# The last tile of a routed expert kernel: its sum and store in three parts instead of two, and two early stores joined

## The chip, the cores and the metric

The kernel runs on one core of a Trainium2 chip. The metric is the device time of one execution in microseconds (us); the profile's own times are given in us from the start of its span, single instructions also in nanoseconds (ns). Engines are called as in the profile: PE (TensorE, matmuls), PEld (its weight loads), DVE (VectorE), ACT (ScalarE), POOL (GpSimd) and SP (SyncE, which only issues transfers here). SPq and ACTq are the queues on which SP and ACT issue transfers (DMAs).

## The reference

`x` is 128 batches of 32 tokens with 128 features, float32. First each batch gets a linear layer of its own, a mix of 8 masked matrices; then 2 of 8 experts are chosen per batch, and one shared expert is applied to every token. Both layers are added to their input.

```python
w_bot = einsum('bg,got->bot', cond, weight * mask)
x = x + einsum('bnt,bot->bno', x, w_bot) + bias
# per batch: softmax over cond, the best 2 of 8 experts, weights normalised
out = sum over experts e of we[:, e] * mlp(x, gate[e], up[e], down[e])
out = out + mlp(x, shared_gate, shared_up, shared_down)
x = x + out
# mlp(x, g, u, d) = (gelu(x @ g) * (x @ u)) @ d, hidden width 512
```

## The kernel before

All arrays lie with the features on the 128 partitions and the 4096 tokens along the free axis, as 8 tiles of 512 columns (`TB`); `P` is 128. `x1` holds the output of the first layer, `acc` the running sum of the second one, both with all 4096 columns. The order of work is written out by hand (`manual_schedule`), so that each engine executes its instructions in the order of the code; buffers come from pools that hand them out in turn, and an instruction that takes a buffer again waits until the earlier user of it is done.

The kernel first builds the 128 matrices of the batches and applies them, with the routing computed on DVE beside it. Then it runs MLP tiles: two shared tiles, 27 expert tiles whose tokens are gathered by POOL and whose sums are scattered into `acc` by DVE (L716), and at the end the remaining shared tiles 2 to 7. More expert tiles than 27 are in a branch of `tc.If` (L822); the profiled execution loads 27 sets of expert weights, so it took the `Else` branch, in which `late_tiles` (L807) follows at once. Both branches hold a copy of `late_tiles`.

A shared tile has 4 groups of 128 hidden units. For each, `hidden` (L574) issues the gate and the up matmul (L580, 512 columns each), a GELU on ACT (L585) and a product on DVE (L587) that gives `h`; `down` (L590) multiplies `h` by the down weights into a PSUM bank `ps_out` (L598), accumulating over the 4 groups. `Pipeline.run` (L649) keeps `down` one group behind `hidden`, so that PE has the next group's matmuls while ACT and DVE make `h`; for the last tile the lag is set to 2 (L815). With a lag of 2, the groups 2 and 3 of the last tile are still pending when `run` returns, and the loop behind it issues their `down` matmuls, part by part.

A tile may be given `widths`: then its output columns are cut into parts with a PSUM bank each. The pool `ps_o` (L84) has three banks. When a part's last group is done, `finish` (L659) is called. For shared tiles above number 2 it takes a buffer `o` from a pool of two, adds the bank and `acc` into it on DVE (L668), and stores it (L670):

```python
o_pool = ctx.enter_context(tc.tile_pool(name="o", bufs=2))      # L79
...
o = o_pool.tile([P, w], F32, name="o", tag="o")                 # L667
nc.vector.tensor_tensor(o, ps[:, 0:w], acc[:, cols], ALU.add)
queue = nc.scalar if part.start else nc.sync
queue.dma_start(out=outT[:, cols], in_=o)
```

So tiles 3 to 6 take one `o` buffer each, and the last tile, number 7, takes one for each part: 384 columns, stored on SP's queue, and 128 columns, stored on ACT's. The finished tiles 0 to 2 lie in `acc` itself and are stored from there at the top of `late_tiles`, by two transfers on SP's queue (L810): 1024 columns, and the 512 of tile 2, whose last addition (L665) comes some microseconds later. After that, SP's queue has only the stores of `o`.

At the very end each engine runs through its branch (L822), and SP waits for the last stores (L885).

Of the kernel before, what the change touches and what calls it, by code (L numbers as in the profile page):

```python
# [25 lines left out]
EARLY = 2  # L26
# [4 lines left out]
def kernel(  # L31
# [16 lines left out]
    nc = tc.nc  # L48
    P = 128
# [5 lines left out]
    TB = 512  # L55
    BT = TB // N
    NTILE = NT // TB
# [47 lines left out]
    def warm_up(n):  # L105
# [10 lines left out]
        out=before,  # L116
        in_=ones,
# [38 lines left out]
    acc = const.tile([P, NT], F32, name="acc")  # L156
# [499 lines left out]
    pipe = Pipeline(h_pool)  # L656

    def shared_tile(t, widths=None):
        def finish(ps, part):  # L659
            w = part.stop - part.start  # L660
            cols = slice(t * TB + part.start, t * TB + part.stop)
            if t < EARLY:
                nc.vector.tensor_tensor(acc[:, cols], ps[:, 0:w], x1[:, cols], ALU.add)
            elif t == EARLY:
                nc.vector.tensor_tensor(acc[:, cols], ps[:, 0:w], acc[:, cols], ALU.add)  # L665
            else:
                o = o_pool.tile([P, w], F32, name="o", tag="o")  # L667
                nc.vector.tensor_tensor(o, ps[:, 0:w], acc[:, cols], ALU.add)  # L668
                queue = nc.scalar if part.start else nc.sync
                queue.dma_start(out=outT[:, cols], in_=o)  # L670

        return Mlp(TB, x1[:, ts(t, TB)], shared, finish, widths)
# [133 lines left out]

    def late_tiles(pipe):  # L807
        late.ps = None
        for early in (slice(0, EARLY * TB), ts(EARLY, TB)):
            nc.sync.dma_start(out=outT[:, early], in_=acc[:, early])  # L810
        pipe.run(late, slice(1, None))
        for t in range(EARLY + 2, NTILE - 1):
            pipe.run(shared_tile(t))

        pipe.lag = 2  # L815
        pipe.run(shared_tile(NTILE - 1, (TB - P, P)))
        for part in range(2):
            for mlp, group, h in pipe.pending:
                mlp.down(group, h, slice(part, part + 1))


    with tc.If(n_used > SURE[0], preferred_fallthrough_block=False) as more_tiles:  # L822
        more = Pipeline(h_more_pool)
        for kind in range(3):
            for i in range(SURE[kind], CAPS[kind]):
                more.run(expert_tile(more, kind, i))
        more.drain()
        more.flush()
        late_tiles(pipe.copy())
    with more_tiles.Else():  # L830
        late_tiles(pipe)
# [57 lines left out]
```

## Time and profile before

| what | value |
|---|---|
| median of 3 runs | 285.92 us (285.91 to 286.01) |
| the profiled execution's own time | 285.23 us |
| its span, first to last instruction | 283.3 us |
| mean granted TensorE clock | 0.998 of full |
| PE busy, share of the span | 278.0 us, 98% |
| DVE, ACT, POOL busy | 167.0, 78.9 and 48.1 us |
| transfers | 27.21 MB, of them 2.10 MB written |

The profiled execution took 1.93 us more than its span, which lies ahead of the first and behind the last instruction, and was 0.69 us shorter than the median of the timed runs. In the profile, a matmul in float32 appears as two instructions of PE (and two weight loads), so "x2" of a form is one matmul of the code. "To landing" is the time from the issue of a transfer until its completion is signalled.

### The profile page before, as it was taken

To read this page: it belongs to the slowest core of one execution; us is meant where nothing else is said; L and a number is where in the kernel's file an instruction comes from. 1 tells how busy PE (TensorE), PEld (TensorE's weight loads), DVE (VectorE), ACT (ScalarE), POOL (GpSimd) and SP (SyncE) were. 2 spreads that over 40 slices of the span, in tenths; PEclk is the share of its full clock that TensorE was granted. 3 is DMA by queue.
4 is the path that set the end of the run, shared out by engine and by line. 5 is a ranking of instruction groups with operands and counts; after the bars stand their busy time and mean duration, and the time that the engine had idled before them with its cause. 6 is when DMAs were issued, how large, how long until landed. Compare 5 with 4: busy or idle time off the path is not lost. (4 is left out here: it accounts for less than half of the span.)

```text
span 283.3 us, 5170 instructions
## 1 busy us (share of the span) xinstructions
PE 278.0 (98%) x1424; PEld 172.1 (61%) x1424; DVE 167.0 (59%) x489; ACT 78.9 (28%) x149; POOL 48.1 (17%) x285
## 2 busy tenths in 40 slices
PE   8999999999999999999999999999999999999994
PEld 7987545657657567576675665765557444444442
DVE  4897794546666666666566676666666833233232
ACT  5665123222222222222222222222222222222220
POOL 3001213423024220241222212421000000000000
PEclk9999999999999999999999999999999999999999
DMA  4381068434335335325353343432000020100001
GB/s 121 116 207 58 2 167 278 115 111 118 113 106 170 127 111 150 113 93 167 82 186 106 112 150 111 126 118 94 3 0 1 25 86 0 39 37 11 26 37 46
DMA packets 25763, 27.21 MB, mean 96 GB/s; under 512 B 1920, under 2 KB 16768, under 8 KB 25728
## 3 DMA queue, kind: packets, MB, share of 16 engines
q1 hardware_dynamic: 25440, 26.42, 30.5%
q10 hardware_dynamic: 288, 0.39, 0.5%
q8 instruction: 13, 0.21, 0.3%
q14 instruction: 22, 0.18, 0.2%
HBM read 24.71 MB, written 2.10 MB: 95 GB/s over the span
## 5 line engine op out<-in xcount | busy, mean ns | idle before, releaser
L587 DVE TENSOR_TENSOR h<-ge,pu 128x384 f32<-128x384 f32 (+1 forms) x117 | 69.3, 592 | 76.4 <-PE pu L580 76.4
L585 ACT ACTIVATE ge<-pg 128x384 f32<-128x384 f32 (+1 forms) x117 | 61.4, 525 | 186.1 <-PE pg L580 175.7
L716 DVE SCALAR_TENSOR_TENSOR acc<-ps_out,slot_w,acc 128x32 f32 x260 | 65.2, 251 | 27.5 <-DVE h L587 17.1
L598 PE MATMUL ps_out<-h,wd 128*128 128x384 f32 (+2 forms) x216 | 70.3, 424 | 0.0
L580 PE MATMUL pu<-xg,wu 128*128 128x384 f32 (+2 forms) x216 | 70.0, 423 | 0.0
L580 PE MATMUL pg<-xg,wg 128*128 128x384 f32 (+2 forms) x216 | 70.0, 423 | 0.0
L709 POOL COPY xg<-x 128x32 f32 x260 | 42.1, 212 | 120.1 <-PE pu L580 96.3
L580 PEld LDWEIGHTS pg<-xg,wg 128*128 128x128 f32 x216 | 37.7, 190 | 19.8 <-issue 0.7
L598 PEld LDWEIGHTS ps_out<-h,wd 128*128 128x128 f32 x216 | 37.5, 190 | 20.1 <-DVE h L587 1.3
L580 PEld LDWEIGHTS pu<-xg,wu 128*128 128x128 f32 x216 | 37.7, 190 | 19.1
L580 PE MATMUL pg<-x,swg 128*128 128x512 f32 x64 | 32.8, 594 | 0.0
L580 PE MATMUL pu<-x,swu 128*128 128x512 f32 x64 | 32.7, 592 | 0.0
L598 PE MATMUL ps_out<-h,swd 128*128 128x512 f32 (+2 forms) x72 | 32.4, 545 | 0.0
L598 PEld LDWEIGHTS ps_out<-h,swd 128*128 128x128 f32 x72 | 13.3, 190 | 14.9 <-issue 12.2
L580 PEld LDWEIGHTS pu<-x,swu 128*128 128x128 f32 x64 | 12.2, 190 | 15.3 <-issue 15.1
L580 PEld LDWEIGHTS pg<-x,swg 128*128 128x128 f32 x64 | 11.8, 190 | 12.6 <-issue 11.7
L292 DVE COPY W<-w 128x512 f32<-128x512 f32 x16 | 9.9, 682 | 0.7 <-PE w L278 0.7
L294 ACT COPY W<-w 128x512 f32<-128x512 f32 x16 | 8.3, 597 | 3.7 <-PE w L278 3.7
L278 PE MATMUL w<-yd,wT 32*128 32x128 f32 x256 | 9.0, 279 | 0.0
L278 PEld LDWEIGHTS w<-yd,wT 32*128 32x128 f32 x256 | 8.2, 186 | 1.2 <-DVE x L321 0.8
L325 POOL COPY acc<-x 128x512 f32<-128x512 f32 x6 | 3.7, 616 | 29.7 <-DVE x L321 29.5
L303 PE MATMUL pz<-W,xin 128*32 128x128 f32 x256 | 7.8, 274 | 0.1
(99 smaller groups left out, 68.7 us busy)
## 6 DMA issues: line engine op xcount, KB each, us to landing
wg<-in_gate_dram SPq DMA_DIRECT2D x27, 256.0 KB, 2.7
wu<-in_up_dram SPq DMA_DIRECT2D x27, 256.0 KB, 2.9
wd<-in_down_dram SPq DMA_DIRECT2D x27, 256.0 KB, 3.0
xin<-in_xT_dram SPq DMA_DIRECT2D x6, 256.0 KB, 4.0
out_dram<-o SPq DMA_DIRECT2D x4, 256.0 KB, 2.0
xin<-in_xT_dram SPq DMA_DIRECT2D x1, 512.0 KB, 7.4
out_dram<-acc SPq DMA_DIRECT2D x1, 512.0 KB, 2.6
w_sb<-in_w0T_dram ACTq DMA_DIRECT2D x1, 320.0 KB, 3.1
```

The costliest lines, as they stand in the source:

```text
L278: nc.tensor.matmul(banks[j][:, ts(k, NB * OQ)], wT[rows, q0 + k, :], yd[rows, ts(i, NB), :].rearrange("p b o -> p (b o)"), start=True, sto ...
L292: nc.vector.tensor_copy(dst, src)
L294: nc.scalar.copy(dst, src)
L303: nc.tensor.matmul(pz[j * N : (j + 1) * N, ts(k, P)], x_sb[t][:, ts(b, N)], W[:, t * BT + b, :], start=True, stop=True,)
L325: nc.gpsimd.tensor_copy(acc[:, ts(t, TB)], x1[:, ts(t, TB)])
L580: nc.tensor.matmul(ps[:, ts(i, self.n)], w[:, ts(c, P)], self.x_in, start=True, stop=True,)
L585: nc.scalar.activation(ge[:, 0:n], pg[:, 0:n], AF.Gelu_apprx_tanh)
L587: nc.vector.tensor_tensor(h[:, 0:n], ge[:, 0:n], pu[:, 0:n], ALU.mult)
L598: nc.tensor.matmul(ps[:, 0 : cols.stop - cols.start], self.wd[:, c, :], h[:, i * self.n + cols.start : i * self.n + cols.stop], start=(c = ...
L709: nc.gpsimd.tensor_copy(xg[:, ts(j, N)], x1[:, bass.ds(v, N)])
L716: nc.vector.scalar_tensor_tensor(a, ps[:, ts(j, N)], slot_w[:, slot0 + j : slot0 + j + 1], a, ALU.mult, ALU.add,)
```

## The change

The last tile is cut into three parts of 256, 128 and 128 columns, with a PSUM bank and an `o` buffer each. For the two pending groups, the parts 0 and 1 are issued first, group by group, and then part 2. The queue is chosen by where the part starts: the part from column 256 is stored on ACT's queue, the parts from 0 and from 384 on SP's. The two stores from `acc` become one of 1536 columns, issued when the last addition into tile 2 is done.

```diff
-                queue = nc.scalar if part.start else nc.sync
+                queue = nc.scalar if part.start == TB // 2 else nc.sync
                 queue.dma_start(out=outT[:, cols], in_=o)
...
     def late_tiles(pipe):
         late.ps = None
-        for early in (slice(0, EARLY * TB), ts(EARLY, TB)):
-            nc.sync.dma_start(out=outT[:, early], in_=acc[:, early])
+        early = slice(0, (EARLY + 1) * TB)
+        nc.sync.dma_start(out=outT[:, early], in_=acc[:, early])
         pipe.run(late, slice(1, None))
...
         pipe.lag = 2
-        pipe.run(shared_tile(NTILE - 1, (TB - P, P)))
-        for part in range(2):
+        pipe.run(shared_tile(NTILE - 1, (TB // 2, P, P)))
+        for parts in (slice(0, 2), slice(2, 3)):
             for mlp, group, h in pipe.pending:
-                mlp.down(group, h, slice(part, part + 1))
+                mlp.down(group, h, parts)
```

## Prediction, written before the changed kernel ran

> **What bounds the kernel now.** I read the page's busy row and its row of slices first, then the end of the timeline, then the rows of the last transfers.
>
> ```profile
> PE 278.0 (98%) x1424; PEld 172.1 (61%) x1424; DVE 167.0 (59%) x489; ACT 78.9 (28%) x149; POOL 48.1 (17%) x285
> PE   8999999999999999999999999999999999999994
> ```
>
> PE works through the whole span except for its last slice. So only two things can move the time: the work of PE, and what comes after PE's last matmul. The end, from the timeline (start, duration, engine and line):
>
> ```profile
> 276.42 2.77 PE L598 MATMUL ps_out<-h,swd 128*128 128x384 f32 x12
> 278.78 0.75 DVE L668 TENSOR_TENSOR o<-ps_out,acc 128x384 f32<-128x384 f32 x2 [1.40 <-PE ps_out L598]
> 279.36 0.33 SPq L670 DMA_DIRECT2D out_dram<-o  x1
> 279.56 0.35 ACTq L670 DMA_DIRECT2D out_dram<-o  x1
> ```
>
> PE ends at 276.42 + 2.77 = 279.19. The sum of part 0 runs beside PE's last matmuls, the sum of part 1 follows them, and from 279.56 on there are only two transfers in flight. The transfer view for the last stretch (queue: packets, MB, share; then issues: KB and us to landing) and SP's waits (us, times, longest) say how long they take:
>
> ```profile
> q14 instruction: 4, 0.03, 3.2%
> q8 instruction: 1, 0.02, 1.8%
> ...
> out_dram<-o SPq DMA_DIRECT2D x1, 192.0 KB, 2.9
> out_dram<-o ACTq DMA_DIRECT2D x1, 64.0 KB, 2.8
> ```
> ```profile
> SPq L885 <- DMA out_dram<-o: 1.7, 2, 1.6
> ```
>
> The stores land at 279.36 + 2.9 = 282.26 and 279.56 + 2.8 = 282.36, SP waits for them at L885, and the span ends 0.94 later. This tail of 283.3 - 279.19 = 4.1 us is what the change works on.
>
> **What a store costs.** The rows for other stores, from the page's transfer issues and the tile view of `o`:
>
> ```profile
> out_dram<-o SPq DMA_DIRECT2D x4, 256.0 KB, 2.0
> ...
> out_dram<-acc SPq DMA_DIRECT2D x1, 512.0 KB, 2.6
> ```
> ```profile
> DMA to landing us min/median/max: 2.0/2.4/3.1
> ```
>
> A store of 256 KB lands 2.0 us after its issue (three of the four of `o`), one of 512 KB 2.6. The fourth took 3.1; in its stretch (240.4 to 243.6), as after 279.5, an instruction-queue packet (q8 or q14) runs, and a few data packets come late, long after the rest. In fine windows of the last stretch, q14 packets of some 8 KB stand near 280.4, 281.0 and 281.3 among the data, and the last data packets trickle until 281.8. So I have a clean price (2.0 at 256 KB) and a price for a store that meets instruction packets (2.8 to 3.1).
>
> **The change, part by part.**
>
> *Joined early store.* Before, 1024 columns go at 225.4 and 512 at 230.1, when L665 is done. After, all 768 KB go at 230.1. By the two rows, 0.6 us for each further 256 KB, it lands in about 3.2 us, at 233.3. The next user of SP's queue is the store of tile 3 at 240.4. One issue of 0.35 us on SP goes. Both are hidden by 7 us of PE work in which nothing waits for a transfer: 0. If that cover were gone, it would cost the 0.6 us by which a 768 KB store is longer than one of 512 KB.
>
> *PE work of the last tile.* In each of 4 groups one matmul of 384 columns becomes one of 256 and one of 128, that is 4 matmuls more (8 instructions). From the starts in fine windows, a pair of instructions takes 0.86 us at 512 columns, 0.64 at 384 (276.42 to 277.06), and 0.22 at 128 (277.06 to 277.28). That is linear: a 256 takes 0.43, and 0.43 + 0.22 = 0.65 against 0.64. The weight loads of 0.19 do not show at a pitch of 0.11 in the four 128-column instructions at the end. So 4 x 0.01 = 0.04 us at most, and I count 0.
>
> *The third PSUM bank.* With three banks, the third is that of tile 6, so part 2's first matmul waits for tile 6's sum. In the timeline that sum runs 272.32 to 273.01; part 2's first matmul comes at 273.83 + 0.43 + 0.22 = 274.48. Cover 1.5 us, cost 0. Without the cover PE would stand for what is left of that 0.69 us sum, and the next tile group behind it too.
>
> *The third `o` buffer, a wait that the profile of before does not have.* The pool has two. Tiles 5 and 6 had both, long landed; part 0 takes tile 5's, part 1 tile 6's, part 2 takes part 0's again. In the compiled order the last sum waits for three things: PE, DVE, and the completion of the store of part 0, which was issued just before. Queued behind that wait are the last store on SP and then the end of the kernel; nothing else is on DVE. Worked out on the profile's clock:
>
> - Part 0 (256): the pending loop starts at 277.28. Group 2's parts 0 and 1 take 0.43 + 0.22, so group 3's part 0 runs from 277.93. Its second instruction starts at 278.15 and lasts about 0.38 (between the rows 274 ns for 128 and 486 ns for 384): 278.53. DVE starts 0.05 later, as at 278.73/278.78 before. The sum lies between 280 ns (128 columns) and 558 ns (384): 0.42. Ends 279.00, SP issues at 279.01.
> - Part 1 (128): sum until about 279.2 behind it, ACT issues at 279.2. It lands before the last store in all cases below.
> - Part 2 (128): PE is done at 279.19 as before. The sum waits for part 0's landing at 279.01 + L1. Then 0.05 to start, 0.28 for the sum, 0.02 to the issue: 279.36 + L1. It lands at 279.36 + L1 + L3.
>
> Against the 282.36 of before, the change in the end is **L1 + L3 - 3.00 us**. The new order puts two store latencies behind one another where the old one had them side by side.
>
> *L1 and L3.* Lower bound: both clean, sizes from the two clean rows (1.4 + 0.6 per 256 KB): 128 KB 1.7, 64 KB 1.55, sum 3.25, change +0.25. Upper bound: both as the end pair of before, 2.9 and 2.8, sum 5.7, change +2.7. I take the middle case, one of the two stores meets the instruction packets: 2.9 + 1.55 = 4.45 or 1.7 + 2.8 = 4.5, change **+1.45**. Reason: the packets come as the engines reach the end of their code. PE and ACT still get there at about 279.2 to 279.6, beside part 0's store; DVE and SP now get there only with part 2. So they are likely to be spread over both stores, and each store is smaller than the 192 KB that was hit.
>
> *A page against the row.* The clean row is 2.0 us for 256 KB. The Trainium skill, "DMA: Bandwidth & Descriptors", section "Anatomy of one DMA — SWDGE (gpsimd) path", gives for transfers issued by GpSimd a fit of 2.0 us fixed plus the bytes at 436 GB/s; that would be 2.6 at 256 KB, which this trace undercuts. By the page L1 = 2.3 and L3 = 2.15, and the change would be an estimate of +1.45; by the clean rows +0.25. Its section "Rules for kernel authors" speaks against cutting: join small transfers, under 64 KB is mostly overhead. Here the rows decide the ends of my range; that the page falls on my middle case is by another route.
>
> *Sum.* 0 + 0 + 0 + 1.45. The profiled execution would go from 285.23 to 286.7. It was 0.69 under the median; nothing of that lies in the tail's arithmetic, so I add the same 1.45 to the median: 285.92 + 1.45 = 287.4 us.
>
> **Rivals.**
>
> 1. *Not slower: the two stores in a row are both clean.* The place is DVE's wait before the last sum; the price is L1 + L3 - 3.00, and it decides at L1 + L3 = 3.57 (+0.2%). For it: the stores are small, part 0's is under way earlier than before, and the old 2.8 and 2.9 contain some 1.2 us of delay that need not come back. Against it: instruction packets come at every end of the kernel, and no store in this trace, of any size, landed under 2.0. At 3.25 it gives 286.2 us, within the bound.
> 2. *Faster: the last sum does not wait for a store.* Then part 2 is summed at 279.23 to 279.51, its 64 KB go at 279.53, and land after 1.55 to 2.8: 281.1 to 282.35, a change of -1.3 to 0, about 285.3 us. For it: the parts have other widths, and buffers kept apart by width would not be reused. Against it: one tag and two buffers in L79 and L667, and the compiled wait. For a gain despite the wait L1 + L3 would have to be under 2.43; the first packets of a store appear only some 0.8 us after its issue (280.2 for 279.36), twice that is 1.6 alone.
> 3. *The third bank stalls PE* or the joined store collides: 1.5 us and 7 us of slack speak against both; I fold them into the upper tail.
>
> **How the numbers follow.** What can be told from no change here is about 0.2%, 0.57 us. The chain of two stores with at least one delay: 0.82, likeliest 287.4, from 286.5 (L1 + L3 = 3.57) to 288.6. Rival 1: 0.14, 286.2. Rival 2: 0.04, 285.3. So faster 0.04, same 0.14, slower 0.82. The range goes from just under the clean sum, 286.1, to just over the upper bound, 288.7; it leaves out rival 2 and sums outside the bounds, under 2 in 10.
>
> **What would show it.** The last sum of 128 columns should start some 2 to 3 us after PE's end, idle until a DMA of `out_dram<-o`, not PE; DVE should have two rows at L668 near 278.6 to 279.2 and one near 281 to 282. PE's end should stay within 0.05 us of 279.2, the last 12 instructions at L598 becoming 18. SP's last issue should come at about 279.36 + L1. Nothing should differ before 273 us but the store at 230.1. I am wrong if the third sum starts at PE's end, if PE shows a gap near 274.5, or if both last stores land in about 1.6 us.

## The result, and the profile after

The changed kernel takes 287.40 us (median of 8 runs, 287.09 to 287.96) against 285.92 us for the kernel before: slower, with a ratio of 1.0062, 95% interval 1.0043 to 1.0080.

The end of the changed kernel, from the timeline (start, duration, engine, line, operation; in brackets the idle time before it and what ended that):

```profile
276.96 2.80 PE L598 MATMUL ps_out<-h,swd 128*128 128x256 f32 x18
...
279.13 0.62 DVE L668 TENSOR_TENSOR o<-ps_out,acc 128x256 f32<-128x256 f32 x2 [1.21 <-PE ps_out L598]
279.58 2.67 SPq L670 DMA_DIRECT2D out_dram<-o  x2
279.78 0.35 ACTq L670 DMA_DIRECT2D out_dram<-o  x1
281.60 0.29 DVE L668 TENSOR_TENSOR o<-ps_out,acc 128x128 f32<-128x128 f32 x1 [1.85 <-DMA out_dram<-o]
```

PE is done at 276.96 + 2.80 = 279.76, 2.80 us after its start where it took 2.77 before, although it now executes 18 instructions instead of 12. The first two sums follow as in the kernel before. The third does not: DVE stands idle for 1.85 us, and what ends that is a store, not PE. The row of SP's queue joins two issues, the second at 279.58 + 2.67 - 0.33 = 281.92.

The waits of the last stretch (engine, line, what it waited for: us in total, times, longest) have that row as a new one:

```profile
DVE o L668 <- DMA out_dram<-o: 1.9, 1, 1.9
```

The transfer view from 279.5 on gives the landings, and the instruction packets that run in the same stretch:

```profile
q14 instruction: 4, 0.03, 1.8%
q8 instruction: 1, 0.02, 1.3%
...
out_dram<-o SPq DMA_DIRECT2D x1, 128.0 KB, 1.9
out_dram<-o ACTq DMA_DIRECT2D x1, 64.0 KB, 1.9
out_dram<-o SPq DMA_DIRECT2D x1, 64.0 KB, 2.8
```

So L1 is 1.9 us and L3 2.8 us, one behind the other. The last store lands at 281.92 + 2.8 = 284.7, and the span ends 0.9 later, as before. The page's chain of waits, which broke off behind the last sum before, now has `DMA out_dram<-o` in it, with 1% of the span.

Not all of the 2.3 us between the two spans (285.6 and 283.3) belongs to the change. The sum of L665, ahead of everything that the change touches, is already late (the first row from the profile before, the second from the one after):

```profile
229.40 0.69 DVE L665 TENSOR_TENSOR acc<-ps_out,acc 128x512 f32<-128x512 f32 x1
229.94 0.69 DVE L665 TENSOR_TENSOR acc<-ps_out,acc 128x512 f32<-128x512 f32 x1
```

The first shared matmul is late by as much (20.4 and 21.0), so this half microsecond arises in the first 21 us; what causes it there was not followed. I therefore compare tails, from the start of the last block of `ps_out` matmuls to the end of the span: 283.3 - 276.42 = 6.88 before, 285.6 - 276.96 = 8.64 after, 1.76 us more. L1 + L3 - 3.00 = 1.9 + 2.8 - 3.0 = 1.7 accounts for it.

### The profile page after: what moved, and what is told of

Read it like the earlier page. It is cut to its first block, busy times and chain, and to the rows that moved or that the text cites. A ratio compares the mean times of both kernels' runs of the same rounds, so it can differ in the third digit from the quotient of the medians.

```text
span 285.6 us, 5188 instructions
## 1 busy us (share of the span) xinstructions
PE 278.5 (98%) x1432; PEld 173.6 (61%) x1432; DVE 167.0 (58%) x490; ACT 79.0 (28%) x149; POOL 47.9 (17%) x285
## 4 chain that ended last, share of the span: by engine, by line
PE 97%; DMA 1%; DVE 0%; issue 0%; DVEq 0%
PE pg L580 29%; PE pu L580 29%; PE ps_out L598 29%; PE w L278 3%; PE pz L303 3%; PE warm L107 1%; PE pt L320 1%; DMA out_dram<-o 1%; PE pt L255 1%; PE ps_w L544 0%; DVE o L668 0%; PE ps_y L214 0%; DVE ones L99 0%; PE ps_i L543 0%; PE ps_n L370 0%
## 5 line engine op out<-in xcount | busy, mean ns | idle before, releaser
L598 PEld LDWEIGHTS ps_out<-h,swd 128*128 128x128 f32 x80 | 14.2, 190 | 14.1 <-issue 12.2
```

What stands on the lines that cost most here:

```text
L598: nc.tensor.matmul(ps[:, 0 : cols.stop - cols.start], self.wd[:, c, :], h[:, i * self.n + cols.start : i * self.n + cols.stop], start=(c = ...
```

## Experiments

My theory: the last sum waits for the store of part 0 because it takes that store's buffer again, and two landings in a row are the whole loss. Rivals: cutting in three costs by itself (more PE instructions, more transfers), or the joined early store does. A second question was why the last store takes 2.8 us and the first 1.9. In all runs below the kernel before ran beside the tried one; its median was 285.39 to 285.62 us in these three sets, so each is judged by its ratio.

**Three buffers.** The wait is taken away, all else is kept.

```diff
-    o_pool = ctx.enter_context(tc.tile_pool(name="o", bufs=2))
+    o_pool = ctx.enter_context(tc.tile_pool(name="o", bufs=3))
```

> The changed kernel with three o buffers instead of two, so that the last sum need not wait for the store of part 0. Theory (the two stores one behind the other are the whole loss): the last sum starts at PE's end and the last 64 KB are issued within 0.4 us of it; the 1.5 us are given back, and since the last store is then like that of before, the time is that of before to a few tenths, 285.6 us (285.0 to 286.1). Rival (cutting in three or the joined early store costs, by crowding the queues or more work on PE): it stays near 287.4.

285.47 us, ratio 0.9998 (0.9986 to 1.0010): the whole loss is gone. From the timeline of this run:

```profile
276.44 2.80 PE L598 MATMUL ps_out<-h,swd 128*128 128x256 f32 x18
...
278.61 0.96 DVE L668 TENSOR_TENSOR o<-ps_out,acc 128x256 f32<-128x256 f32 x3 [1.21 <-PE ps_out L598]
279.06 0.87 SPq L670 DMA_DIRECT2D out_dram<-o  x2
```

and from its transfer view the landing of the last store:

```profile
out_dram<-o SPq DMA_DIRECT2D x1, 64.0 KB, 2.5
```

The three sums are one row now, without a gap, done at 279.57. The last issue on SP is at 279.06 + 0.87 - 0.33 = 279.60, and the tail is 283.4 - 276.44 = 6.96 us, as before (6.88). So cutting in three costs nothing that can be told, and it brings nothing either: PE's end, one sum of 0.28 and one store of 64 KB are the same last steps in both cuts.

**The joined store alone.** The kernel before with this part of the change only.

```diff
-        for early in (slice(0, EARLY * TB), ts(EARLY, TB)):
-            nc.sync.dma_start(out=outT[:, early], in_=acc[:, early])
+        early = slice(0, (EARLY + 1) * TB)
+        nc.sync.dma_start(out=outT[:, early], in_=acc[:, early])
```

> The kernel before with only the two early stores joined. Theory: the joined store lies beside more than 7 us of PE work and nothing waits for it: no change, 285.9 us to within 0.3. Rival (the later and longer store is part of the loss): 286.4 or more.

285.57 us, ratio 1.0001 (0.9992 to 1.0011): no change. The joined store of 768 KB landed in 3.2 us, beside matmuls.

**One buffer, the changed kernel.** The suspected wait is doubled: `bufs=1` in the same line.

> The changed kernel with one o buffer: the sum of part 1 now waits for the store of part 0, and that of part 2 for the store of part 1, three landings in a row instead of two. Theory: another landing of 1.9 us and a sum with its issue, 0.35 us: 2.2 us more than the changed kernel, 289.6 us (289.2 to 290.5); the sums of the earlier tiles find the buffer free, as their stores are about 10 us apart. Rival (the wait in the changed kernel is not what costs): it stays near 287.4.

289.80 us, ratio 1.0143 (1.0117 to 1.0169); 2.4 us over the changed kernel's median (2.3 by the two ratios), where 2.2 were expected. Both sums behind the first now wait for a store:

```profile
278.65 0.42 DVE L668 TENSOR_TENSOR o<-ps_out,acc 128x256 f32<-128x256 f32 x1 [1.21 <-PE ps_out L598]
279.10 5.49 SPq L670 DMA_DIRECT2D out_dram<-o  x2
280.98 0.29 DVE L668 TENSOR_TENSOR o<-ps_out,acc 128x128 f32<-128x128 f32 x1 [1.90 <-DMA out_dram<-o]
281.30 0.35 ACTq L670 DMA_DIRECT2D out_dram<-o  x1
283.94 0.29 DVE L668 TENSOR_TENSOR o<-ps_out,acc 128x128 f32<-128x128 f32 x1 [2.68 <-DMA out_dram<-o]
```

**One buffer, the kernel before.** `bufs=1` in the kernel before, cut in 384 and 128 as it was. Nothing else of the change is in it.

> The kernel before, cut in two parts as it was, with one o buffer: the sum of the last 128 columns must wait for the store of the 384. Nothing else of the change is in it. Theory: the end moves by L1 + L3 - 2.64 us (issue at 279.36, 0.36 for start, sum and issue of the second, 282.36 before); with 1.9 and 2.8 us as in the changed kernel 2.1 us more, 288.0 us (286.7 to 288.9). Rival (the third part is what costs): no change, 285.9 us.

287.31 us, ratio 1.0064 (1.0039 to 1.0090): within the range expected, below its middle, and the same as the whole change costs. The last sum waits for the store of part 0 here too, where in the kernel before it followed the first one at once:

```profile
281.43 0.29 DVE L668 TENSOR_TENSOR o<-ps_out,acc 128x128 f32<-128x128 f32 x1 [2.01 <-DMA out_dram<-o]
```

The stores took 1.9 and 2.7 us, so the formula gives 1.9 + 2.7 - 2.64 = 1.96 us; the tail is 285.3 - 276.50 = 8.80, that is 1.92 more than before. The wait alone makes the loss, with two parts as with three.

**Part by part.** Part 0 is finished before part 1 begins.

```diff
-        for parts in (slice(0, 2), slice(2, 3)):
+        for parts in (slice(0, 1), slice(1, 2), slice(2, 3)):
```

> The changed kernel, two o buffers, but the pending matmuls go part by part: both groups of part 0 first, then both of part 1, then both of part 2. Theory: part 0 is done by the 0.22 us of group 2's part 1 earlier, its store starts as much earlier, and the last sum with it: about 0.2 us less than the changed kernel, 287.2 us (286.9 to 287.5); the chain of two stores is not shortened. Rival (the end is set by PE or by the last part's own matmuls): no change at all, 287.4, and the third sum would not move with the first store.

287.51 us, ratio 1.0061 (1.0040 to 1.0081): no gain. The first step happened: the first sum starts 1.95 us after the start of the last PE block (277.26 and 279.21) instead of 2.17 (276.96 and 279.13). In the profiled execution the first store then took 2.3 us instead of 1.9, and the third sum, which again waited for it (2.12 us idle, ended by `out_dram<-o`), came 0.16 us later against PE's block than in the changed kernel. The interval of the ratio is 0.6 us wide to each side, so these runs cannot tell whether the expected 0.2 us is there in the mean.

**The branches the other way round.** The second question. In the code, the branch that runs stands first, and each engine jumps over the other one at its end. With the order turned, the branch that runs is the last code, and the jump lies at the If. The branch records of the weight loads' queue show it (first the kernel before, then the same kernel with the order turned):

```profile
L822 PEldq COMPARE_BRANCH  x2: 95/1960/3826, 226.8 to 277.4; - x2
L822 PEldq COMPARE_BRANCH  x1: 3558/3558/3558, 227.5 to 227.5; - x1
```

Before, the branch at the If takes 95 ns and a second one, at 277.4, takes 3.83 us; turned, there is only the one at the If, and that takes 3.56 us. The queues of the other engines, too, have two branches before and one with the order turned. The turned order was tried on the changed kernel, on the kernel before, and with three buffers, by one edit:

```diff
-    with tc.If(n_used > SURE[0], preferred_fallthrough_block=False) as more_tiles:
+    with tc.If(n_used > SURE[0], preferred_fallthrough_block=True) as more_tiles:
```

> The changed kernel with the two branches laid out the other way round: the branch that runs is the last code of the program, so nothing is jumped over at the end, but the jump into it comes at the If. Theory (instruction packets at the jump delay the last stores): q14 and q8 packets no longer stand among the last stores, the last 64 KB land in 1.9 us instead of 2.8, 0.9 us less at the end, and PE may pay 0 to 2 us at the If: PE's gap shows by its start of the last tile. Landing of the last store 1.6 to 2.0. Rival (a small store at the end takes 2.5 to 2.8 for another reason): landing stays 2.5 to 2.8.

> The kernel before with the branches laid out the other way round. Theory (instruction packets): the two last stores land in about 1.9 to 2.0 us instead of 2.8 and 2.9, 0.9 us less at the end; with 0 to 2 us paid by PE at the If the time is 284.6 to 286.6 us. Rival: landings stay 2.8 and 2.9, and the time is that of before or more.

> Three o buffers as in the run with three buffers, and the branches the other way round. If both theories hold it is the best end: last store issued at 279.5, landed 1.6 to 1.9 later at 281.2, which is 1.1 us less than before at the end, less what PE pays at the If (0 to 2 us): 284.4 to 286.4 us. Rival (the landing is not set by the instruction packets): the time of before plus what PE pays.

The transfer view from 278 on, for the changed kernel with the order turned:

```profile
q14 instruction: 1, 0.01, 0.2%
...
out_dram<-o SPq DMA_DIRECT2D x1, 128.0 KB, 1.8
out_dram<-o ACTq DMA_DIRECT2D x1, 64.0 KB, 1.8
out_dram<-o SPq DMA_DIRECT2D x1, 64.0 KB, 1.5
```

and for the kernel before with the order turned:

```profile
q14 instruction: 1, 0.01, 0.2%
...
out_dram<-o SPq DMA_DIRECT2D x1, 192.0 KB, 1.9
out_dram<-o ACTq DMA_DIRECT2D x1, 64.0 KB, 1.9
```

All but one of the instruction packets at the end are gone, and with them the long landings: 1.5 where the changed kernel had 2.8, 1.9 and 1.9 where the kernel before had 2.9 and 2.8. The packets now stand at the If. Between 226 and 234 the kernel before has none; with the order turned it has these, and the early store that they meet lands in 3.9 us instead of 2.0:

```profile
q8 instruction: 2, 0.03, 1.9%
q14 instruction: 3, 0.02, 1.0%
...
out_dram<-acc SPq DMA_DIRECT2D x1, 256.0 KB, 3.9
```

In the changed kernel and with three buffers the joined store of 768 KB landed in 5.2 us with the order turned, where it took 3.2 in the changed kernel. Nothing waits for these early stores. The price appears at the If, as idle time of the weight loads and of the matmuls there. From the waits of the kernel before with the order turned (226 to 240 us):

```profile
PEld pg L580 <- issue: 3.9, 9, 1.9
...
PE pg L580 <- issue: 1.1, 1, 1.1
```

How much that is can be read from two rows of its timeline, L665 and the last block of `ps_out` matmuls:

```profile
230.11 0.69 DVE L665 TENSOR_TENSOR acc<-ps_out,acc 128x512 f32<-128x512 f32 x1
...
278.50 2.77 PE L598 MATMUL ps_out<-h,swd 128*128 128x384 f32 x12
```

The stretch between their starts is 48.39 us, where it was 276.42 - 229.40 = 47.02. In the same way for the other kernels, in us:

| kernel | L665 to the last PE block | tail | sum against its own original |
|---|---|---|---|
| before | 47.02 | 6.88 | |
| before, order turned | 48.39 | 5.90 | +1.37 - 0.98 = +0.39 |
| changed | 47.02 | 8.64 | |
| changed, order turned | 48.33 | 7.30 | +1.31 - 1.34 = -0.03 |
| three buffers | 47.03 | 6.96 | |
| three buffers, order turned | 48.65 | 5.72 | +1.62 - 1.24 = +0.38 |

The timed runs agree: 285.94 us, ratio 1.0014 (1.0007 to 1.0021) for the kernel before with the order turned, 287.43 us, 1.0063 (1.0044 to 1.0082) for the changed kernel, and 285.95 us, 1.0010 (0.9999 to 1.0020) with three buffers. What the end gains, the If takes, and in two of the three kernels some 0.4 us more.

**All last stores on SP's queue.** An attempt to have the one without the other: with no store to issue, ACT reaches the end of its code early, and its instruction packet should run before the stores.

```diff
-                queue = nc.scalar if part.start else nc.sync
+                queue = nc.sync
```

> The kernel before with the last 128 columns stored on SP's queue too, so that ACT has no store to wait for and comes to the end of its code after its last GELU, some 3 us earlier. Theory: ACT's instruction packet goes out before the last stores; the second store is issued 0.13 us later (behind SP's issue of 0.33). If ACT's packet was the one that delayed the stores, they land in about 2.0 us and 0.6 us are gained, 285.0 us; if it was DVE's or SP's own, landings stay 2.5 to 3.2 and the time is that of before to within 0.3, 285.6 us. Either way one q14 packet less stands after the last issue.

> Three o buffers, with all three last stores on SP's queue. The issues come one behind the other, 0.33 us each, the last at about 0.13 us later than with ACT's help. Theory as for the kernel before with all stores on SP: landing of the last store about 1.7 us and 0.6 to 0.8 us gained over before (284.8 us) if ACT's packet was the one that delayed, else the time of before (285.5 us) to within 0.3.

In the kernel before with all stores on SP, one q14 packet ran before 279.4 already, but one stayed between 279.4 and 280.5, one q14 and one q8 packet between 281.5 and 282.5, and the landings stayed too. Its transfer view from 278 on:

```profile
q14 instruction: 3, 0.02, 0.8%
...
out_dram<-o SPq DMA_DIRECT2D x1, 192.0 KB, 2.7
out_dram<-o SPq DMA_DIRECT2D x1, 64.0 KB, 2.5
```

285.47 us, ratio 1.0002 (0.9994 to 1.0010), and 285.47 us, 1.0006 (0.9994 to 1.0018) with three buffers, whose last store landed in 2.2 us. It was not ACT's packet alone. No kernel of this study is faster than the kernel before.

## Why the prediction was right

The changed kernel is slower by the mechanism that was named, and by about the amount. That the median is the predicted 287.4 to the first decimal is luck: the tail grew by 1.76 us where 1.45 was predicted, and the ratio of 1.0062, taken from 285.92, makes it 1.8 us too. Step by step:

- *The wait and its place.* Right: the third sum idles 1.85 us for `out_dram<-o`. That this wait is the loss is shown by three runs: with three buffers the loss is gone, with one buffer it more than doubles, and the kernel before gets it too when it is given one buffer.
- *L1 + L3 - 3.00.* Right to 0.1 us, 1.7 for a tail that is 1.76 us longer. The same form, with 2.64, gave 1.96 for a measured 1.92 in the kernel before with one buffer.
- *L1 and L3.* The sum, 4.7 us, was 0.2 above the 4.5 of the middle case. The clean price of a 128 KB store was set too low by the line through 256 and 512 KB: 1.7, where 1.8 and 1.9 were measured. The clean 64 KB was well placed: 1.55, and 1.5 to 1.9 measured with the order of the branches turned. The fit in the Trainium skill, "DMA: Bandwidth & Descriptors", section "Anatomy of one DMA — SWDGE (gpsimd) path", which is for transfers from GpSimd, is above every one of these: an estimate of 2.15 for 64 KB and 2.3 for 128 KB.
- *Where the instruction packets fall.* My reason was wrong here. I expected them to be spread over both stores. In the changed kernel none started while the stores of parts 0 and 1 moved their data (280.0 to 281.5); they came from about 281.6 on, around the last store. One store clean and one hit was the right count, with the first clean; but it was taken as the middle between two bounds, and the reason given for it does not hold, so it came out in part by luck.
- *The costs put at nothing.* PE's last block grew by 0.03 us, where 0.04 at most was worked out. No PE gap shows at the third bank. The joined store alone made no difference, and landed in the 3.2 us given.
- *Rival 1, both stores clean*, is not what happened; the changed kernel with the order turned shows it at the end (1.8 and 1.5: 0.3 us by the formula, a tail 0.42 longer than before), where the If takes the gain away. *Rival 2, no wait*, was excluded by the code; the run with three buffers shows what it would have been worth: the time of before, which is the upper end of what I gave it, since its last store still meets instruction packets (2.5 us).

The medians differ by 1.48 us where the tails of the two profiles differ by 1.76; that gap is smaller than what the median of the kernel before moved from set to set (285.39 to 285.92), and here the kernel before stood at the upper end of that.

## What to carry to other kernels

Count the buffers against the parts when the last tile of a kernel is cut: a pool with one buffer too few ties the last sum to the landing of a store that was issued a moment ago, and even 64 KB took at least 1.5 us to land here. Cutting the last store smaller brought nothing by itself, since PE's end, one short sum and one landing remain. At the end of a program, look for instruction packets among the last stores: here they went with a jump at the end of the code, and the last 64 KB landed 0.8 to 1.3 us later beside them. Moving the jump elsewhere moved its price with it.

## What the runs showed of the hardware that was not expected

- Stores that had instruction packets beside them landed later. In every kernel that had the packets at its end, the last store of 64 KB took 2.2 to 3.2 us, and 1.5 to 1.9 without them; in the kernel before the difference is 0.9 us. With the order turned the packets stood at the If, and there the early store took 3.9 instead of 2.0 us. That the packets belong to the jump is shown by the turned order, which moves both together. How a packet holds up a store is not shown.
- A jump in the middle of PE's work is no cheaper. The queue of the weight loads spends 3.3 to 3.8 us in the long branch, in either place; at the end nothing of PE waits for it, and at the If 1.3 to 1.6 us of PE's time go.
